# Moving the second half of a depthwise convolution from its own stage into the scan of the first half of the images

## The chip, the cores and the metric

The kernel runs on one core of a Trainium2 chip. The metric is device time in microseconds (us) for one execution: the median of three runs is 3259.85 us (3253.21 to 3263.72). TensorE (PE in the profile, with PEld for its weight loads) does the matrix products into PSUM, ScalarE (ACT) and VectorE (DVE) read PSUM and SBUF, GpSimd (POOL) works in SBUF, and SyncE (SP) issues most of the DMAs. "PEclk" is the TensorE clock that the throttle granted, as a share of full speed.

## The reference, cut to what matters

The input is 32 images of 96 channels, 56 by 56, in float32. Two layers follow each other.

```
# layer 0
h = depthwise_conv7x7(x) + conv_b
h = layernorm over channels (g, b)
x = x + layer_scale * (gelu(h @ w1 + b1) @ w2 + b2)
# layer 1
x  = silu(depthwise_conv5x5(x) + conv_b)              # "the second convolution"
d, B, C = split(x_proj_w @ x)                         # 6 + 4 + 4 rows
delta   = softplus(dt_w @ d + dt_b)
log_dA  = max(delta * A, log(1e-9))                   # 4 states per channel
P  = exp(cumsum(log_dA along the 3136 positions))
hs = P * cumsum(delta * B * x / max(P, 1e-9))
y  = sum over states of hs * C + x * Ds
```

The two layers meet only through the image: the scan of an image needs the second convolution of that image and of no other.

## The kernel before

The 32 images are two groups of 16 (g = 0 and 1). A convolution block (`conv`) is 4 channels of the 16 images of one group, so 24 blocks make one convolution of one group, and the blocks are numbered n = 0 to 95: 0 to 47 for the 7x7 convolution of both groups, 48 to 71 for the 5x5 convolution of group 0, 72 to 95 for that of group 1. A depthwise convolution is done on TensorE as products with banded matrices: the image rows lie on 32-partition quarters, and for each of the k + 1 column shifts `convolve` (L341) issues 8 products of 32 rows by 64 columns over up to 448 positions, on 4 row groups times 2 column groups of the array, so that a 5x5 block has 48 products (96 instructions in the profile, since each float32 product is two) into one PSUM slot of 4 banks. `bands` (L366) writes the banded matrices of a block on ACT from a table that is built once. `conv_load` (L400 for the 5x5) brings the block in with 8 DMAs on the SP queue; `conv` evicts on ACT, and `put2` (L439) writes the result to DRAM (`conv2_d`) with 4 DMAs on the POOL queue.

The stages follow each other on TensorE. First comes the 7x7 convolution of group 0. Then 56 units (u) of the channel MLP, two per 8 rows of images: `expand` (L569), GELU, `second` (L588) and `residual`, which writes its rows of `block_d`. The units of group 0 also carry the 7x7 convolution of group 1, one block per unit, and the units u = 30 to 49 of group 1 carry one 5x5 block of group 0 each (n = 48 to 67, "mixed" units); TAIL = 4 holds the last four back. After the last unit comes a stage of 28 blocks, n = 68 to 95, that holds nothing else ("the tail"). Then the scan runs, over 32 images with 6 units each (3 channel thirds g times 2 halves h of the columns), 192 units in all.

Each iteration i of the scan loop issues in program order, which every engine keeps:

```
load(p, s)      # SP: 12 DMAs; in two of 12 iterations (a pair of images)
prepare(b, s)   # i mod 6 = 5: project (24 products, px L831, xd); 0: delta (pz L848, softplus);
                # 1, 2: delta_x (POOL product L863, 4 DMAs on SP)
fetch(i+4)      # SP: u <- dx_d, 784 KB
spread(.., 0)   # i mod 6 = 3, 4: pk L879, bc L883 on ACT
decay(i+2)      # PE pd L901, ACT relu L906 twice, ACT exp L910 -> da
drive(i+2)      # POOL u <- u, bc (L915)
spread(.., 1)   # i mod 6 = 5, 0
scan(i)         # DVE L920, L924, L928
weigh(i-1)      # POOL da <- u, bc (L935)
gather(i-2)     # PE py L942, L947; ACT copy y L953; every third: 4 DMAs on SP
```

All products of the scan but none of its state go through one PSUM pool (`banks`) of 2 slots of 2 banks each; the other 4 banks hold the running product `run_t`. So TensorE can be at most two slots ahead of ACT, which empties every slot. The tiles `bc` have 3 buffers for each of the two kinds, `dx` two, `u` six, `da` five.

## Time and profile before

| | before |
|---|---|
| median of 3 runs | 3259.85 us |
| the profiled execution's own time | 3265.01 us |
| its span, first to last instruction | 3263.2 us |
| busy, share of the span: PE, DVE, ACT, POOL | 88%, 66%, 62%, 54% |
| last MLP product ends / tail runs on TensorE | 1296.2 us / 1296.2 to 1476.8 us |
| first scan instruction on DVE | 1511.3 us |
| scan unit 81 starts on DVE / last one starts | 2240.0 us / 3243.4 us |

The shares are means over stages of different kinds. Up to 1296 us TensorE is busy nearly all the time and VectorE is not; from 1511 us on VectorE is busy nearly all the time. The slices of the page show the two, and the windows and timelines of the trace show what happens inside a unit.

### The profile page before, as it was taken

Reading aid. Unit: us, or ns where it says so; the run is one execution under the profiler, and the core shown is the slowest. Engines: PE = TensorE matmul, PEld = TensorE weight load, DVE = VectorE, ACT = ScalarE, POOL = GpSimd, SP = SyncE. Lnnn points to the kernel's source line nnn. Section 1 sums busy time; section 2 is a strip of 40 time slices with the busy share of each in tenths; the row PEclk is TensorE's granted clock in tenths of the full one; section 3 lists DMA queues with packets and bytes.
Section 4 is the critical chain, followed back from the end, with each engine's and each line's share of the span. In section 5 each row is a group of like instructions: output and inputs, shape, how many; then the busy total and the mean of one; then the engine's idle time right before and its main releaser. Section 6 shows DMA issues by size and latency. Waiting matters only on the chain.

```text
span 3263.2 us, 65714 instructions
## 1 busy us (share of the span) xinstructions
PE 2855.5 (88%) x28044; PEld 1058.7 (32%) x28044; DVE 2138.3 (66%) x1226; ACT 2011.3 (62%) x1952; POOL 1760.3 (54%) x901
## 2 busy tenths in 40 slices
PE   8999999999999999887888887888787878887885
PEld 7654444444444444442222222222222222222221
DVE  6654333343121112004999999999999999999998
ACT  7765554444666665445766666666666666666673
POOL 2310111100111111335988898899888988898896
PEclk9999999999999999997788777877887878778786
DMA  8988666544777773997365546554655565556542
GB/s 193 254 244 222 186 183 185 166 129 126 202 206 203 202 200 98 279 275 199 119 179 147 148 149 178 148 151 146 178 149 142 155 175 142 143 163 159 157 156 72
DMA packets 363795, 563.63 MB, mean 173 GB/s; under 512 B 221904, under 2 KB 292576, under 8 KB 363504
## 3 DMA queue, kind: packets, MB, share of 16 engines
q1 hardware_dynamic: 336452, 432.37, 49.1%
q0 software_dynamic: 25424, 127.03, 13.1%
q8 instruction: 221, 3.62, 0.5%
q14 instruction: 70, 0.57, 0.1%
q10 hardware_dynamic: 1628, 0.04, 0.0%
HBM read 355.58 MB, written 203.69 MB: 171 GB/s over the span
## 4 chain that ended last, share of the span: by engine, by line
PE 51%; DVE 16%; ACT 9%; POOL 7%; DMA 7%; SPq 5%; issue 4%; POOLq 0%; DVEq 0%; ACTq 0%
PE pc L341 12%; PE ph L569 12%; PE po L588 12%; DVE u L928 6%; DVE run_t L920 6%; DVE run_t L924 3%; POOL da L935 3%; PE px L831 3%; PE py L947 3%; PE pz L848 3%; ACT da L906 3%; POOL u L915 3%; PE py L942 2%; ACT da L910 2%; PE pd L901 2%
## 5 line engine op out<-in xcount | busy, mean ns | idle before, releaser
L915 POOL TENSOR_TENSOR u<-u,bc 128x1568 f32<-128x1568 f32 x192 | 674.4, 3513 | 209.3 <-DMA u<-dx_d 209.3
L920 DVE TENSOR_TENSOR_SCAN run_t<-da,run_t 128x1568 f32<-128x1568 f32 x192 | 664.5, 3461 | 72.6 <-ACT da L910 54.0
L935 POOL TENSOR_TENSOR da<-u,bc 128x1568 f32<-128x1568 f32 x192 | 674.3, 3512 | 23.1 <-DVE u L928 21.0
L906 ACT ACTIVATE da<-pd,lift_t,a_t 128x784 f32<-128x784 f32 x384 | 378.4, 1003 | 73.1 <-PE pd L901 63.9
L901 PE MATMUL pd<-dl,rep_t 32*128 32x392 f32 x1536 | 388.6, 640 | 33.9 <-ACT bc L883 14.1
L569 PE MATMUL ph<-h,w1c_t 32*128 32x448 f32 x4032 | 398.0, 543 | 7.3 <-DVE o L600 3.8
L588 PE MATMUL po<-g,w_t 128*32 128x448 f32 x4032 | 390.4, 540 | 0.0
L942 PE MATMUL py<-xs,dsm_t 32*32 32x392 f32 x1536 | 250.2, 731 | 147.0 <-ACT bc L883 113.2
L341 PE MATMUL pc<-xc,we 32*64 32x432 f32 (+2 forms) x6912 | 359.3, 554 | 6.7 <-ACT we L366 4.3
L924 DVE SCALAR_TENSOR_TENSOR run_t<-run_t,u 128x1568 f32<-128x1568 f32 x192 | 345.6, 1800 | 21.8 <-POOL u L915 1.5
L575 ACT ACTIVATE g<-ph,b1p_t 128x1792 f32<-128x1792 f32 x168 | 294.5, 1754 | 98.8 <-PE ph L569 95.9
L879 PE MATMUL pk<-xd,pick_t 32*128 32x392 f32 x1024 | 266.0, 632 | 101.4 <-ACT y L953 85.6
L928 DVE TENSOR_TENSOR_SCAN u<-da,u,run_t 128x1568 f32<-128x1568 f32 x96 | 334.1, 3480 | 3.4
L555 DVE TENSOR_TENSOR h<-h,po 128x448 f32<-128x448 f32 x123 | 69.1, 617 | 405.6 <-PE po L588 308.0
L928 DVE TENSOR_TENSOR_SCAN u<-da,run_t 128x1568 f32<-128x1568 f32 x96 | 328.3, 3420 | 3.3
L439 POOL DMA_DIRECT2D conv_d<-ht x192 | 101.3, 535 | 408.6 <-ACT ht L446 268.2
L910 ACT ACTIVATE da<-da,lift_t 128x1568 f32<-128x1568 f32 x192 | 307.9, 1604 | 5.6
L947 PE MATMUL py<-da,sel_t 128*32 128x392 f32 x1536 | 246.7, 728 | 53.5 <-POOL da L935 53.4
L608 POOL DMA_DIRECT2D block_d<-o x112 | 60.2, 562 | 416.5 <-DVE o L600 395.4
L422 POOL DMA_DIRECT2D conv_d<-ht x96 | 57.1, 600 | 406.0 <-ACT ht L420 399.5
L953 ACT COPY y<-py 128x392 f32<-128x392 f32 x192 | 92.1, 480 | 296.3 <-PE py L947 227.0
L569 PEld LDWEIGHTS ph<-h,w1c_t 32*128 32x128 f32 x4032 | 198.8, 185 | 206.5 <-issue 167.3
(123 smaller groups left out, 3092.3 us busy)
## 6 DMA issues: line engine op xcount, KB each, us to landing
u<-dx_d SPq DMA_DIRECT2D x192, 784.0 KB, 5.2
conv_d<-ht POOLq DMA_DIRECT2D x96, 448.0 KB, 6.1
conv_d<-ht POOLq DMA_DIRECT2D x192, 224.0 KB, 5.7
h<-conv_d SPq DMA_DIRECT2D x336, 112.0 KB, 3.0
x<-in_x_dram SPq DMA_DIRECT2D x112, 336.0 KB, 8.6
block_d<-o POOLq DMA_DIRECT2D x112, 336.0 KB, 6.3
xs<-conv_d SPq DMA_DIRECT2D x384, 98.0 KB, 4.1
dx_d<-dx SPq DMA_DIRECT2D x256, 147.0 KB, 3.3
```

The lines of the kernel that those rows point to most:

```text
L341: pin(nc.tensor.matmul(pv[:, :, lo:hi], lhsT=wt[rows, j, k - d], rhs=xv[rows, j, :, lo + e : hi + e, s], start=(t == 0), stop=(t == k), ti ...
L569: pin(nc.tensor.matmul(ph[:, q, :TOK], lhsT=w1c_t[quarter(q), e, f * 128 : (f + 1) * 128], rhs=ht[quarter(q), e, s], start=(e == 0), stop= ...
L588: pin(nc.tensor.matmul(po[quarter(q), e, :TOK], lhsT=w2_t[:, f, e * PR : (e + 1) * PR], rhs=gts[u, f][:, q], start=(f == 0), stop=(f == 2) ...
L901: pin(nc.tensor.matmul(ps[:, j, :BK], lhsT=rep_t[quad(q)].rearrange("p c n -> p (c n)"), rhs=dls[b, h][quad(q), g], start=True, stop=True, ...
L906: pin(nc.scalar.activation(pair(da, a), ps[:, :, :BK], AF.Relu, bias=lift_t[:, 0:1], scale=a_t[:, g : g + 1],))
L910: pin(nc.scalar.activation(da, da, AF.Exp, bias=lift_t[:, 1:2], scale=1.0))
L915: pin(nc.gpsimd.tensor_mul(us[i], us[i], bcs[b, h, 0]))
L920: pin(nc.vector.tensor_tensor_scan(run_t[:, 1 : T + 1], da, zero, run_t[:, T : T + 1] if h else 1.0 / EPS, ALU.mult, ALU.add,))
L924: pin(nc.vector.scalar_tensor_tensor(run_t[:, :T], in0=run_t[:, 1 : T + 1], scalar=1.0, in1=ut, op0=ALU.min, op1=ALU.mult,))
L928: pin(nc.vector.tensor_tensor_scan(ut, da, run_t[:, :T], last["h"] if h else 0.0, ALU.mult, ALU.add))
L935: pin(nc.gpsimd.tensor_mul(das[i], us.pop(i), bcs[b, h, 1]))
L947: pin(nc.tensor.matmul(py[quad(j)], lhsT=sel_t, rhs=hc[:, j * BK : (j + 1) * BK], start=False, stop=True, tile_position=(0, j * PR),))
```

## The change

The constant TAIL goes away, so the MLP units u = 30 to 53 carry all 24 blocks of group 0. The tail is removed. The 24 blocks of group 1 (n = 72 to 95) are issued inside the scan of group 0, as 48 half blocks of two row groups each, at the end of the iterations with i mod 6 in 1, 2, 4 and, for even images, also 3. The first half of a block is copied out of PSUM (ACT), the second is evicted with SiLU, and SiLU is then applied to the first (ACT). The half blocks take their PSUM slot from the scan's `banks`. Their matrices are written to DRAM on the POOL queue when those of group 0 are made (the two groups have the same matrices), and each block's 393 KB come back by one SP DMA into a single buffer; the block's 8 loads and the 4 DMAs of its result are on the SP queue too. In the scan's loop the second `spread` comes one iteration later, `bc` has 2 buffers instead of 3 and `dx` one instead of two. Constants that only the first stages need move to a pool that is given back.

```diff
-XB, HB, TAIL = 4, 2, 4
+XB, HB = 4, 2
...
+    bands_d = [dram.tile([128, 2 * (K2 + 1) * 2 * PR], F32, name=f"bands_d{k}") for k in range(KB)]
...
-    def convolve(ps, xt, wt, k):
+    def convolve(ps, xt, wt, k, lanes=range(Q)):
...
-            for i in range(Q):
+            for i in lanes:
...
-                    pv = ps[j * 64 : (j + 1) * 64, i, :TOK].rearrange("p (b g) -> p b g", b=BI)
+                    pv = ps[j * 64 : (j + 1) * 64, i - lanes[0], :TOK].rearrange("p (b g) -> p b g", b=BI)
...
         wes[n] = t
+        if n >= half_n:
+            pin(nc.gpsimd.dma_start(bands_d[kb], t.rearrange("p j d m -> p (j d m)")))
...
-        mixed = 0 < u < half_u and n1 < half_n or u >= half_u + 2 and n2 < half_n + KB - TAIL
+        mixed = 0 < u < half_u and n1 < half_n or u >= half_u + 2 and n2 < half_n + KB
...
-    late = convs.enter_context(tc.tile_pool(name="late", bufs=1))
-    more += [late.tile([128, 2, COLS], F32, name=f"xd_{i}") for i in range(4)]
-    for t in more:
-        nc.vector.memset(t, 1.0)
-    last = half_n + KB
-    for n in range(n2, 2 * half_n):
-        ahead(n, last if n < last - XB else 2 * half_n)
-        conv(n)
...
-            dx = apool.tile([128, NG, BK], F32, name=f"dx_{k}", tag="dx")
+            dx = apool.tile([128, NG, BK], F32, name=f"dx_{k}", tag="dx", bufs=1)
...
-            t = pool.tile([128, T], F32, name=f"bc{i}_{b}_{h}", tag=f"bc{i}", bufs=3)
+            t = pool.tile([128, T], F32, name=f"bc{i}_{b}_{h}", tag=f"bc{i}")
...
+        xqs = [late.tile([128, 2, COLS], F32, name=f"xq_{i}") for i in range(2)]
+        blocks = range(half_n + KB, 2 * half_n)
+        halves = [(n, c) for n in blocks for c in range(2)]
...
+        def bring(n):
+            if n in blocks:
+                conv_load(n, xqs[n % 2])
+
+        def bring_bands(n):
+            if n in blocks:
+                t = late.tile([128, 2, K2 + 1, 2 * PR], F32, name=f"wq_{n}", tag="bands", bufs=1)
+                pin(nc.sync.dma_start(t.rearrange("p j d m -> p (j d m)"), bands_d[n % KB]))
+                wes[n] = t
+
+        def half_block(n, c):
+            ps = banks(f"pc_{n}_{c}")
+            convolve(ps, xqs[n % 2], wes[n], K2, range(2 * c, 2 * c + 2))
+            if c == 0:
+                hqs[n] = late.tile([128, Q, TOK], F32, name=f"hq_{n}", tag="ht", bufs=1)
+                pin(nc.scalar.copy(hqs[n][:, :2], ps[:, :, :TOK]))
+            else:
+                ht = hqs.pop(n)
+                pin(nc.scalar.activation(ht[:, 2:], ps[:, :, :TOK], AF.Silu))
+                pin(nc.scalar.activation(ht[:, :2], ht[:, :2], AF.Silu))
+                wes.pop(n)
+                coming.append((n + 2, n + 1))
+                leaving.append((n, ht))
...
+        bring_bands(blocks[0])
+        bring(blocks[0])
+        bring(blocks[1])
         for i in range(units + 3):
...
             if 0 <= i + 4 < units:
                 fetch(i + 4)
+            out_now, leaving[:] = leaving[:], []
+            if coming:
+                bring_bands(coming[0][1])
+                bring(coming.pop(0)[0])
...
-            b, s = divmod(i + 1, PER)
-            if i and b < B and s < 2:
+            b, s = divmod(i, PER)
+            if b < B and s < 2:
                 spread(b, s, 1)
-            if i == 0:
-                spread(0, 0, 1)
-                spread(0, 1, 1)
...
             if 0 <= i - 2 < units:
                 gather(i - 2)
+            for n, ht in out_now:
+                put2(n, ht, nc.sync)
+            b, s = divmod(i, PER)
+            if halves and (s in (1, 2, 4) or s == 3 and b % 2 == 0):
+                half_block(*halves.pop(0))
```

## The prediction

> **What bounds the kernel now.** I read the page's busy shares and slices first.
>
> ```profile
> PE 2855.5 (88%) x28044; PEld 1058.7 (32%) x28044; DVE 2138.3 (66%) x1226; ACT 2011.3 (62%) x1952; POOL 1760.3 (54%) x901
> PE   8999999999999999887888887888787878887885
> DVE  6654333343121112004999999999999999999998
> PEclk9999999999999999997788777877887878778786
> ```
>
> There are two regimes. Up to slice 19 TensorE is full at full clock; from 1511 us VectorE is full, and the clock falls. The windows of the scan's units 0 to 80 and 81 to 191 put numbers to it (columns: busy us of PE, PEld, DVE, ACT, POOL, each with its count; clock; DMA share; GB/s):
>
> ```profile
> 1511.00:2240.00 729.00, 600.75 (x3670) 162.65 (x3670) 705.55 (x244) 493.44 (x557) 637.22 (x189) 0.79 0.58 158
> 2240.00:3252.00 1012.00, 806.01 (x4900) 215.46 (x4900) 966.64 (x333) 657.95 (x740) 871.69 (x257) 0.79 0.53 150
> ```
>
> VectorE is busy 97% and 96% of the time, so a unit costs 9.0 to 9.1 us and an image (6 units) 54.4. But nothing else is loose: PE 82%, POOL 87%, ACT 68%. The waits show how near the others are.
>
> ```profile
> ACT y L953 <- PE py L947: 227.0, 117, 8.6
> POOL u L915 <- DMA u<-dx_d: 209.3, 31, 9.6
> PE py L942 <- ACT bc L883: 113.2, 62, 2.7
> PE pk L879 <- ACT y L953: 85.6, 45, 6.5
> DVE run_t L920 <- ACT da L910: 54.0, 24, 32.6
> PE py L947 <- POOL da L935: 53.4, 18, 6.1
> ```
>
> PE waits for ACT to empty a PSUM slot, and ACT for PE to fill one: a chain that goes to and fro over two slots. It waits for its pace-setter (POOL's da, which follows the scan) only 53 us in all on PE. How fast the chain goes when nothing holds it can be read from ACT's timeline, from the start of one exp (L910) to the next. For the six units of an image the distances that recur are 4.0, 5.9, 5.9, 9.7 (a px in between), 14.3 (a pz and both table loads) and 8.3 us: 48.1 us. So the chain has about 6 us of slack per image, and that is all the room the change has. A plain unit is ACT back to back:
>
> ```profile
> 2017.68 1.90 ACT L906 ACTIVATE da<-pd,lift_t,a_t 128x784 f32<-128x784 f32 x2 [0.51 <-PE pd L901]
> 2019.62 1.61 ACT L910 ACTIVATE da<-da,lift_t 128x1568 f32<-128x1568 f32 x1
> 2021.13 0.46 ACT L953 COPY y<-py 128x392 f32<-128x392 f32 x1
> ```
>
> **Part 1, the tail goes.** It runs from 1296.2 us (end of the last MLP product) to 1476.8, and the first scan instruction comes at 1511.3: 215.1 us from the MLP's end to the scan. Four of its 28 blocks become mixed units. PE's timeline of the MLP's last mixed unit and of the plain one after it:
>
> ```profile
> 1190.34 4.99 PE L341 MATMUL pc<-xc,we 32*64 32x448 f32 x96
> 1195.25 7.05 PE L569 MATMUL ph<-h,w1c_t 32*128 32x448 f32 x72
> 1202.13 0.91 PE L546 MATMUL po<-rstd_t,pickr_t 32*128 32x448 f32 x2
> 1202.97 6.97 PE L588 MATMUL po<-g,w_t 128*32 128x448 f32 x72
> 1209.87 7.05 PE L569 MATMUL ph<-h,w1c_t 32*128 32x448 f32 x72
> ```
>
> A block is 4.91 us there (1190.34 to 1195.25) in a full PE: 4 x 4.91 = 19.6 us. What remains between the MLP's end and the first scan is the loading of xs, project, delta, spread and decay. Before, it took 41.7 us from the first xs issue (1469.6) to 1511.3. The loads may have to wait until the last unit's o is written out, 12 us after the MLP (1308.2). I take 45 us, between 38 and 54. The scan then starts at 1296.2 + 19.6 + 45 = 1361, **150 us sooner** (141 to 157). The 24 matrix stores add 24 POOL issues of about 0.56 us in a stage where POOL is 15% busy: nothing; uncovered it would be 13 us.
>
> **Part 2, the half blocks.** A tile of the array takes its products one after another. ph has 72 instructions on four tiles, 18 in a row on each, in 6.88 us: 0.38 us per step. The whole pc block has 96 on eight tiles, 12 in a row, in 4.91: 0.41. A half block keeps two row groups, so 48 instructions on four tiles: still 12 in a row. It takes 4.6 to 4.9 us, as long as a whole block; I take 4.7 at full clock, and 4.7 / 0.79 = 5.9 at the scan's. That is 48 x 4.7 = 226 us of PE work in units 1 to 80, in place of 24 x 4.9 = 118.
>
> ACT adds per block one half copy and two half SiLUs (whole tiles took 1.65 and 1.68, so 0.84 each) and two table loads (1.28 each): 5.1 us, 2.5 per half block.
>
> The SP queue gets 13 issues per block (8 loads, one for the matrices, four of put2, which leave POOL): 312 at 0.43 to 0.53 us, some 150 us in about 930, with the 68 per pair of images that it has. By itself that fits, as do 2.2 MB per block, 57 GB/s on top of 158; what counts is the order, below. The two memsets of the new input tiles (1.55 us each on VectorE) lie in the 45 us of Part 1.
>
> Where does it lie? In a plain unit pc gets its slot when the second relu is gone and py is issued, some 4 us into the unit. The unit's exp and y pass under pc, so those 4.7 us come on top of the 4.0. The eviction after it finds the next unit's pd in the other slot waiting for the same ACT: a copy delays it by about 0.3, two SiLUs by about 1 more, and the exp's table load, where no pc covers it, by 1.28. Averaged: 0.8. The matrices have one buffer and can only be fetched when the second half's last product is done; they land about 5.2 us after issue (the median of the 784 KB u), and the next pc in a plain unit is ready after some 4. The result tile has one buffer too: 8 load issues (0.43 each) and put2's four lie before its landing (5.7), about 12 us after the SiLU's half block ended, while the next copy is ready after 9 to 11. In four images 4 of 7 blocks follow directly, and one of them finds the 12 xs loads (6.3 to 9.2 us) ahead on the SP queue. I put this at 7 us per four images, 0.5 per half block.
>
> So 6.0 us per half block, between 4.7 (all but the product hidden) and 9.5 (clock stays at 0.79: 5.9, ACT 1.6, DMA waits 2.0). With 3.5 per image the chain becomes 48.1 + 21.0 = **69.1 us per image** (64.6 to 81.4), well above VectorE's 53.8: VectorE waits. A busier PE may be granted more clock: px and pz (5.9 and 4.9 us for 48 instructions) would shrink to 4.2 each, and the lower end becomes 62. Units 0 to 80 are 13.5 images: 13.5 x 69.1 = 933 us against 729: **204 us lost** (108 to 370).
>
> **Part 3, the rest of the scan.** The later second spread takes about 2.5 us out of the longest stretch (px to pz) and puts it in a short one. With two bc buffers the first spread's eviction waits for the last drive on the buffer (POOL, issued one iteration before), and the relus queued behind it wait too; the weigh that gather waits for anyway follows on POOL 3.5 us later, so at worst 3 us per image. With one dx buffer POOL waits for the first dx's DMAs (3.3 us to landing, plus queueing behind xs loads) before the second, and behind it wait drive and weigh, but POOL already stands 209 us for u. I take +10 us for the 18.5 images after unit 81, between -15 and +40.
>
> **Sum.** Against the profiled execution (3265.0 us with 1.8 outside its span, 5.2 above the median): -150 + 204 + 10 = +64, so 3329. Against the median: 3260 + 64 = 3324 us.
>
> Break-even is at (729 + 150 - 10) / 13.5 = 64.4 us per image, or 4.7 us per half block: precisely the product alone. All else would have to be hidden.
>
> **Two rules of the Trainium skill.** Row: from 2030 to 2044 us the clock was 0.52 with PE busy 11.0 of 14 us and no gap over 2.7 us. "TensorE: Matmul & The Clock Gate" (HAM oscillation) asks only that PE not idle for more than about 3.4 us; the row disagrees. By the rule the new chain would run at full clock: 45.5 + 21 = 66.5 us per image, and 3289 us. Row: pc to ph (32x64 to 32x128 tiles) passes at 1195.25 without a gap. "TensorEngine Tiling (Array Packing)" (Key Properties) says that a change of tiling mode drains the array, which speaks against putting pc between py and pd; at an estimated 0.16 us (a product's 0.54 less its step of 0.38), two per half block, it would add 15 us.
>
> **Rivals.**
> *Faster:* PE at full clock (px and pz at 4.2: chain 45.5) with ACT and DMA hidden: 45.5 + 3.5 x 4.9 = 62.6 per image, 845 us for units 0 to 80: 3260 - 150 + 116 + 5 = 3231, with a quiet second half. For it: the tail ran at 0.86 to 0.97 in its windows of 50 us, and pc fills the very gaps that dropped the clock. Against it: 227 us of ACT waiting for PE and 199 of PE waiting for ACT (113.2 + 85.6) already show a chain that does not overlap. It decides below 64.4 us per image.
> *Much slower:* the single buffers and the SP queue. Each block pays its matrix fetch and put2 in full, and the clock stays at 0.79: 8 us per half block, 76.1 per image: +298 - 150 + 20 gives 3428. For it: SP already waits 481 us for y and 552 for da and u. Against: fetches are issued four units ahead.
> *Hidden:* the half blocks fit under VectorE and the whole 150 stays: 3120. Against it stands the 6 us of slack.
>
> **How the numbers follow.** Forecast (3275 to 3390) 0.56, much slower 0.13, faster 0.24, hidden 0.03, nothing 0.04. Measurement of this kernel tells about 0.3% from no change. Faster 0.27, same 0.04, slower 0.69. The range leaves out the hidden case and the ends of the two outer ones: 3205 to 3440; the forecast's own is 3275 to 3390.
>
> **What would show it.** Right: the scan starts near 1361; pc of 48 takes 4.7 to 6 us; DVE is below 85% busy up to unit 80 at some 11.5 us per unit and back at 9.1 after, with the wait for the exp (L910) grown from 54 to some 200 us; ACT's silus find their table loaded under pc. Wrong: DVE stays above 93% in units 1 to 80; or POOL or SP, not the PE and ACT chain, ends DVE's waits; or the second part of the scan changes by over 40 us.

## The result, and the profile after

The changed kernel takes 3547.5 us (median of four runs, 3542.64 to 3562.04) against 3261.78 us for the kernel before beside it: a ratio of 1.0887, with a 95% interval of 1.0845 to 1.0928. It is slower by 286 us where 64 were forecast. The profiled execution spans 3541.7 us, 278.5 more than before.

The page of the changed kernel, busy shares and three rows of the slices:

```profile
PE 3141.2 (89%) x28044; PEld 1126.1 (32%) x28044; DVE 2134.9 (60%) x1224; ACT 2064.1 (58%) x2015; POOL 1728.0 (49%) x829
PE   8999999999999988988998899899887878877885
DVE  6654333431111114555666656565799999999998
PEclk9999999999999996666676857566677777777786
```

TensorE runs the same 28044 products, but is busy 286 us longer (2855.5 before). The stretch in which VectorE is half idle, slices 15 to 27, is the stretch in which the granted clock shows 5 to 8, mostly 6. The windows of units 0 to 80 and 81 to 191 (span, then busy us of PE, PEld, DVE, ACT, POOL, clock, DMA share, GB/s):

```profile
1364.00:2501.00 1137.00, 1006.35 (x5856) 302.53 (x5856) 705.08 (x243) 610.66 (x668) 640.39 (x188) 0.66 0.56 147
2501.00:3541.00 1040.00, 824.01 (x5024) 228.94 (x5024) 967.01 (x334) 661.06 (x749) 875.46 (x258) 0.75 0.54 148
```

The scan starts at 1363.5 us, 148 sooner than before (1511.3). Units 0 to 80 take 1137.6 us in place of 728.7: 409 lost. The rest takes 1040.6 in place of 1023.2: 17 lost. -148 + 409 + 17 = 278, the difference of the spans. So all of the question lies in the first window, and there the row can be read as a sum. Of TensorE's 1006.35 us the half blocks have this (the same window, instructions that write pc only: PE, PEld, ACT):

```profile
1364.00:2501.00 1137.00, 361.16 (x2208) 123.41 (x2208) 41.93 (x46) 0.66 0.56 147
```

That is 46 half blocks at 7.85 us. The scan's own products took 1006.35 - 361.16 = 645.2 us, where they took 600.75 before, and TensorE was idle for 130.7 us, where it was idle for 128.3. So the lost 409 us are 361 of half blocks, 44 of scan products that became slower, and 2 of idle time: the half blocks filled none of TensorE's gaps, on balance, and all of it is TensorE's busy time.

The waits (us in total, times, longest) that answer to those shown of before:

```profile
DVE run_t L911 <- ACT da L901: 487.7, 76, 40.6
POOL dx L854 <- DMA dx_d<-dx: 244.5, 31, 13.9
ACT y L944 <- PE py L938: 203.2, 107, 8.5
ACT hq L983 <- PE pc L343: 202.5, 23, 18.0
PE py L933 <- ACT bc L874: 109.1, 62, 2.7
PE pc L343 <- DMA wq<-bands_d: 27.3, 3, 10.1
```

VectorE's wait for the exp grew from 54.0 to 487.7 us. ACT waits 202.5 us for first halves alone: it isn't late, it stands behind TensorE. Only 27 us of TensorE's idle time are put down to the matrices' DMA.

Why a half block takes 7.85 us is seen in TensorE's timeline around 2070 us, and in the window of the same stretch:

```profile
2072.91 2.77 PE L892 MATMUL pd<-dl,rep_t 32*128 32x392 f32 x8
2075.69 1.53 PE L933 MATMUL py<-xs,dsm_t 32*32 32x392 f32 x8
2077.15 1.53 PE L938 MATMUL py<-da,sel_t 128*32 128x392 f32 x8
2078.61 9.02 PE L343 MATMUL pc<-xq,wq 32*64 32x448 f32 x48
2087.57 2.78 PE L870 MATMUL pk<-xd,pick_t 32*128 32x392 f32 x8
```
```profile
2051.00:2125.00 74.00, 71.68 (x348) 20.82 (x352) 43.49 (x15) 32.13 (x35) 41.20 (x12) 0.50 0.63 156
```

TensorE is busy 71.68 of 74 us, and yet it has half the clock all through. A half block takes 9.02 us there, and 4.96 at full clock (2025.08 us). The records of the granted clock know only these two levels, and between the first and the last record each lasts a whole number of steps of 3.41 us. In units 0 to 80 of before, half clock adds up to 311 us, and its longest stretch is 13.7 us; in the changed kernel it is 768 us, with twelve stretches over 25 us, the longest 85.3.

ACT's timeline in the same place, to be held against the plain unit shown before:

```profile
2076.77 1.60 ACT L901 ACTIVATE da<-da,lift_t 128x1568 f32<-128x1568 f32 x1
2078.75 0.49 ACT L944 COPY y<-py 128x392 f32<-128x392 f32 x1 [0.38 <-DMA xs<-conv_d]
2079.26 1.28 ACT L986 ACT_TABLE_LOAD   x1
2087.71 0.92 ACT L986 ACTIVATE hq<-pc 128x896 f32<-128x896 f32 x1 [7.17 <-PE pc L343]
2088.52 0.94 ACT L987 ACTIVATE hq<-hq 128x896 f32<-128x896 f32 x1
...
2094.01 1.28 ACT L901 ACT_TABLE_LOAD   x1
```

SiLU's table is loaded while pc runs, as the forecast had it, and ACT then waits 7.17 us more for pc. The exp's table load at 2094.01 is not covered.

### The profile page after: what moved, and what is told of

Same layout as the page of the kernel before. It is cut to its first block, busy times and chain, and to the rows that moved or that the text cites. A ratio compares the mean times of both kernels' runs of the same rounds, so it can differ in the third digit from the quotient of the medians.

```text
span 3541.7 us, 65641 instructions
## 1 busy us (share of the span) xinstructions
PE 3141.2 (89%) x28044; PEld 1126.1 (32%) x28044; DVE 2134.9 (60%) x1224; ACT 2064.1 (58%) x2015; POOL 1728.0 (49%) x829
## 4 chain that ended last, share of the span: by engine, by line
PE 65%; ACT 15%; DVE 5%; SPq 5%; issue 4%; DMA 4%; POOL 2%; POOLq 0%; ACTq 0%; DVEq 0%
PE pc L343 20%; PE po L585 11%; PE ph L566 11%; ACT da L897 5%; PE pd L892 5%; PE px L822 4%; PE py L933 4%; PE py L938 4%; ACT da L901 3%; PE pk L870 3%; SPq L803 2%; ACT dl L846 2%; DVE u L919 2%; ACT bc L874 2%; DVE run_t L911 2%
## 5 line engine op out<-in xcount | busy, mean ns | idle before, releaser
L911 DVE TENSOR_TENSOR_SCAN run_t<-da,run_t 128x1568 f32<-128x1568 f32 x192 | 664.5, 3461 | 500.5 <-ACT da L901 487.7
L892 PE MATMUL pd<-dl,rep_t 32*128 32x392 f32 x1536 | 405.4, 719 | 75.3 <-ACT bc L874 61.1
L343 PE MATMUL pc<-xq,wq 32*64 32x432 f32 (+1 forms) x2304 | 379.2, 825 | 37.3 <-DMA wq<-bands_d 27.3
L854 POOL TENSOR_TENSOR dx<-dl,xs 128x1176 f32<-128x1176 f32 x64 | 189.5, 2960 | 416.0 <-DMA dx_d<-dx 244.5
L933 PE MATMUL py<-xs,dsm_t 32*32 32x392 f32 x1536 | 262.6, 766 | 138.4 <-ACT bc L874 109.1
L919 DVE TENSOR_TENSOR_SCAN u<-da,u,run_t 128x1568 f32<-128x1568 f32 x96 | 334.1, 3480 | 3.4
L919 DVE TENSOR_TENSOR_SCAN u<-da,run_t 128x1568 f32<-128x1568 f32 x96 | 328.4, 3420 | 3.3
L870 PE MATMUL pk<-xd,pick_t 32*128 32x392 f32 x1024 | 276.5, 700 | 29.5 <-ACT da L897 25.2
L938 PE MATMUL py<-da,sel_t 128*32 128x392 f32 x1536 | 254.2, 749 | 25.5 <-POOL da L926 25.5
L892 PEld LDWEIGHTS pd<-dl,rep_t 32*128 32x128 f32 x1536 | 153.3, 244 | 340.8 <-ACT bc L874 141.8
L422 POOL DMA_DIRECT2D conv_d<-ht x96 | 57.3, 602 | 405.8 <-ACT ht L420 395.5
```

The costliest lines, as they stand in the source:

```text
L343: pin(nc.tensor.matmul(pv[:, :, lo:hi], lhsT=wt[rows, j, k - d], rhs=xv[rows, j, :, lo + e : hi + e, s], start=(t == 0), stop=(t == k), ti ...
L892: pin(nc.tensor.matmul(ps[:, j, :BK], lhsT=rep_t[quad(q)].rearrange("p c n -> p (c n)"), rhs=dls[b, h][quad(q), g], start=True, stop=True, ...
L911: pin(nc.vector.tensor_tensor_scan(run_t[:, 1 : T + 1], da, zero, run_t[:, T : T + 1] if h else 1.0 / EPS, ALU.mult, ALU.add,))
L919: pin(nc.vector.tensor_tensor_scan(ut, da, run_t[:, :T], last["h"] if h else 0.0, ALU.mult, ALU.add))
L933: pin(nc.tensor.matmul(py[quad(j)], lhsT=dsm_t[quad(j), g], rhs=tokens(b, h, quad(j), g), start=True, stop=False, tile_position=(j * PR, j ...
L938: pin(nc.tensor.matmul(py[quad(j)], lhsT=sel_t, rhs=hc[:, j * BK : (j + 1) * BK], start=False, stop=True, tile_position=(0, j * PR),))
```

## Experiments

The theory was that the products of the half blocks, which keep two of TensorE's four row groups, are what holds the clock down; the rivals were the loads (SP queue, single buffers), the table loads and evictions on ACT, and the changed order of the rest of the scan. A single run is good to some 10 us (the four runs of the changed kernel lie within 20).

**What of the inserted work costs.** Whole blocks in place of half blocks: 24 blocks, eight tiles on four row groups each, into both slots, SiLU straight out of PSUM, at i mod 6 = 2 and 4 of images 0 to 11.

```diff
-            if halves and (s in (1, 2, 4) or s == 3 and b % 2 == 0):
-                half_block(*halves.pop(0))
+            if waiting and s in (2, 4):
+                whole_block(waiting.pop(0))
```

> The 24 blocks of the second half are issued whole, two per image (i mod 6 = 2 and 4, images 0 to 11), on all eight 32x64 tiles of the array at once, each taking both PSUM slots of the scan; their loads, the fetch of their matrices, the single buffers and the SP queue stay as in the changed kernel, and only one pass of SiLU per half is left. Theory A (a half block fills only half of the array; work of that kind does not get the full clock granted, so pc takes about 8 us instead of 4.7 and the scan's own products slow down with it): pc takes 5 to 6 us per whole block, the granted clock in the scan of the first half is above 0.72 instead of 0.65, a block adds 8 to 10 us to the chain, and the time is 3230 to 3340 us. Theory B (the SP queue and the single buffers): the order of the DMAs is the same, so the time stays above 3450 us. Theory C (SiLU and table loads on ScalarE): the table loads stay, the copies go, so 3480 us or more.

Measured: 3289.16 us (3285.08 to 3296.62), ratio 1.0085 (1.0059 to 1.0112). The window of units 0 to 80 of this run, first all instructions, then pc alone:

```profile
1364.00:2270.00 906.00, 744.27 (x5952) 245.28 (x5952) 704.49 (x243) 590.02 (x648) 640.55 (x188) 0.81 0.71 185
1364.00:2270.00 906.00, 141.94 (x2304) 80.16 (x2304) 41.41 (x48) 0.81 0.71 185
```

The clock is 0.81 in place of 0.66, a whole block takes 5.9 us where two halves took 15.7, and the scan's own products are back at 602.3 us. Of the 286 us, 258 are gone with the same loads, the same table loads and the same buffers. But the run changes the number of products per us, the number of evictions and the rows at once, so it says what is to be looked for, not which of these it is.

Then the rivals by themselves. Without the loads: only the first two blocks are loaded and one set of matrices fetched; the other blocks are computed from these.

```diff
-            if n in blocks:
+            if n in blocks[:2]:
                 conv_load(n, xqs[n % 2])
...
-            if n in blocks:
+            if n in blocks[1:]:
+                wes[n] = wes["kept"]
+            elif n in blocks:
```

> The changed kernel, but only the first two blocks of the second half are loaded and only the first one's matrices are fetched; all blocks reuse them (this leaves out the data of the other 22 blocks). The results are still written out. Theory A (half array, low clock): only the waits of pc for matrices and loads go (37 us of PE idle time ahead of pc in the profile), so 3490 to 3540 us. Theory B (SP queue and single buffers): most of the loss of units 0 to 80 beyond the prediction goes, so below 3400 us.

Measured: 3502.97 us, 44 less than the changed kernel; the clock in units 0 to 80 is 0.68.

Without SiLU: copies in its place, so its table loads and those that bring the exp's table back after it are left out.

```diff
-                pin(nc.scalar.activation(ht[:, 2:], ps[:, :, :TOK], AF.Silu))
-                pin(nc.scalar.activation(ht[:, :2], ht[:, :2], AF.Silu))
+                pin(nc.scalar.copy(ht[:, 2:], ps[:, :, :TOK]))
+                pin(nc.scalar.copy(ht[:, :2], ht[:, :2]))
```

> The changed kernel, but the half blocks of the second half are copied instead of put through SiLU (this leaves out SiLU for half of the images), so the two table loads per block go and the ACT work itself stays. Theory A: the table loads lie mostly under pc, at most 24 x 2.57 = 62 us are saved, so 3480 to 3545 us. Theory C (ScalarE's tables set the pace): below 3420 us.

Measured: 3468.68 us, 79 less; the clock is 0.75. That is more than the 62 us that the table loads themselves could give by the first of the two forecasts, and well short of the second. Both edits together:

> The changed kernel with copies in place of SiLU and with only the first two blocks' loads and one matrix fetch (outputs of the other blocks are left out). Alone, copies gave 79 us and no loads gave 44. Theory (what is left is the product on a clock that is not won back): 3425 to 3455, pc 6.2 to 6.8 us per half block, clock 0.72 to 0.77, still 165 us or more above the kernel before. Rival (tables and DMA waits make the gaps in which the clock is lost): without them the clock holds, pc is 5 to 5.5 us per half block, 3300 to 3380.

Measured: 3434.02 us. The window of units 0 to 80 of this run, all instructions, then pc alone:

```profile
1364.00:2401.00 1037.00, 921.27 (x5856) 270.62 (x5856) 705.13 (x243) 550.22 (x622) 641.08 (x188) 0.73 0.50 133
1364.00:2401.00 1037.00, 301.87 (x2208) 98.16 (x2208) 41.69 (x46) 0.73 0.50 133
```

Loads and tables together account for 113 us. With neither of them 175 us of the loss are still there, and a half block still takes 6.6 us, so the larger part has another cause. The table below sets the runs side by side: the window of units 0 to 80, TensorE's busy time in it, split in pc and the rest, and its idle time.

| kernel | window us | PE busy | pc | scan's own | PE idle | clock |
|---|---|---|---|---|---|---|
| before | 729 | 600.75 | 0 | 600.75 | 128 | 0.79 |
| changed | 1137 | 1006.35 | 361.16 | 645.2 | 131 | 0.66 |
| no loads | 1101 | 990.72 | 349.40 | 641.3 | 110 | 0.68 |
| no SiLU | 1065 | 910.16 | 296.21 | 614.0 | 155 | 0.75 |
| neither | 1037 | 921.27 | 301.87 | 619.4 | 116 | 0.73 |
| whole blocks | 906 | 744.27 | 141.94 | 602.3 | 162 | 0.81 |

The loads are worth 20 us of idle time and 16 of TensorE's busy time. The table loads are worth nothing in idle time; what goes with them is 96 us of TensorE's busy time (65 in pc, 31 in the scan's own), that is, clock. That the holes which the table loads make are where the clock is lost is a reading of this row; no run isolates it.

**Where the clock comes from.** The tail of the kernel before is the cleanest place for this, because TensorE does nothing else there. First its blocks issued as two halves of two row groups, one after the other:

```diff
-        convolve(ps, source(n), wes.pop(n), k)
+        wt = wes.pop(n)
+        if n >= half_n + KB - TAIL:
+            for c in range(2):
+                convolve(ps, source(n), wt, k, range(2 * c, 2 * c + 2))
...
```

> The kernel before, with its tail of 28 blocks in place, but each of these blocks issues its products as two halves of two row groups one after the other (same products, same slot, same evictions). Nothing else is disturbed, so this measures the half width by itself. Theory A: the clock of the tail falls from 0.86 to 0.97 to 0.5 to 0.7 and a block takes 14 to 18 us, the tail 400 to 500 us, and the time is 3480 to 3590 us. Theory A' (half width only halves the number of tiles at work; TensorE is busy without gaps, so the clock stays full): a block takes 9.4 to 9.8 us, the tail about 275 us, and the time is about 3355 us.

Then both halves on the same two row groups, so that they cannot overlap (the second half reads the first's rows, so its output is not the convolution's):

```diff
-                rows = slice(i * PR, (i + 1) * PR)
+                q = i if len(lanes) == Q else i % 2
+                rows = slice(q * PR, (q + 1) * PR)
...
-                        tile_position=(i * PR, j * 64),
+                        tile_position=(q * PR, j * 64),
```

> The kernel before with its tail of 28 blocks, each issued as two halves, and both halves on the same two row groups of the array (the second half computes the first half's rows again, so this leaves out half of the rows of the second half of the images). So only four tiles, 64 of the 128 rows of the array, are ever at work in the tail, with as many products as before. Theory A, sharpened by the run with halves on different rows (whose halves overlapped, PE 100% busy at a clock of 1.00): products on half of the rows do not win the full clock back once it has been lost. The waits for the first blocks of the second half drop the clock, as in the kernel before, and then a block takes about 18 us instead of 9.4: the tail is 400 to 490 us, its clock 0.5 to 0.65, the time 3480 to 3570 us. Theory A' (a TensorE without gaps gets the full clock whatever its tiles): 28 x 9.4 = 263 us, clock above 0.9, the time about 3345 us.

Measured: 3262.68 us, no change, and 3338.05 us. For the first run neither forecast came true, since both took it that the halves would not overlap; in the second the rival's did (about 3345), the theory's (3480 to 3570) did not. The windows of the tail, of the first run and of the second:

```profile
1298.00:1470.00 172.00, 172.00 (x2517) 78.20 (x2513) 8.08 (x7) 85.46 (x80) 54.85 (x104) 1.00 0.87 262
```
```profile
1296.00:1550.00 254.00, 254.00 (x2581) 100.35 (x2576) 8.09 (x7) 88.64 (x82) 56.98 (x108) 1.00 0.76 194
```

In the first the halves overlap across the row groups (6.1 us per block). In the second they follow each other at 9.4 us per block, and the clock is 1.00 for 254 us. So four tiles on two row groups *hold* a full clock as long as TensorE has no gap: a theory by which they always run at half clock falls here. What is left is that they can't win back a clock that has been lost. The second run can't show this, because nothing in its tail makes TensorE wait. For this a gap is needed. 200 tiny operations on ACT ahead of one block's matrices make one, once with the blocks of before and once with those of the run just shown:

```diff
         ahead(n, last if n < last - XB else 2 * half_n)
+        if n == last + 4:
+            for _ in range(200):
+                table(AF.Silu)
         conv(n)
```

> The kernel before, with 200 tiny operations on ScalarE ahead of the matrices of one block in the middle of the tail, so that TensorE runs dry once for 20 us or more; all blocks keep their 8 tiles on all four row groups. Theory (a full clock, once lost, is not won back by products on half the rows, but is by products on all of them): the clock falls to about 0.5 in the gap and is back above 0.95 within about 15 us of products after it; blocks after it take 5 to 6 us each; time 3262 plus the gap, some 3280 to 3310. Rival (any TensorE without gaps wins the clock back): the same. Rival (the clock depends on what ScalarE or the power of the whole core does): no rule for the return.

> The same gap in the tail, where the blocks are issued as two halves one after another on the same two row groups (9.4 us per block at full clock, 3338 us without the gap). Theory: before the gap the clock is 1.00 and a block takes 9.4 us; after it the clock stays near 0.5 for tens of us although TensorE has no gaps, blocks take up to 18 us, and the time is 3420 to 3560. Rival (any TensorE without gaps wins the clock back within some 15 us): 9.4 us per block again after the gap, and 3355 to 3390.

Measured: 3284.75 us and 3519.59 us. TensorE idles 41.05 us at a stretch in the first and 33.57 in the second. The windows of the gap and after, with the eight-tile blocks:

```profile
1358.00:1400.00 42.00, 0.95 (x13) 0.14 (x3) 0.00 (x0) 36.70 (x172) 0.61 (x2) 0.55 0.40 65
1400.00:1410.00 10.00, 10.00 (x137) 8.27 (x145) 0.00 (x0) 5.14 (x5) 3.61 (x7) 0.67 0.71 197
1410.00:1420.00 10.00, 10.00 (x213) 9.19 (x204) 0.00 (x0) 7.03 (x8) 4.21 (x8) 1.00 0.97 253
```

and with the blocks on two row groups:

```profile
1386.00:1430.00 44.00, 10.65 (x109) 4.12 (x100) 0.00 (x0) 38.38 (x181) 0.30 (x1) 0.67 0.24 42
1430.00:1742.00 312.00, 311.78 (x1709) 157.97 (x1713) 0.00 (x0) 57.15 (x54) 39.77 (x76) 0.50 0.43 104
```

This is the cause in one line: 311.78 us busy out of 312, and the clock stays at 0.50 to the end of the tail, while eight tiles have it back within 10 us. In the same run the clock comes back at 1752.2 us, 4 us after the scan's first products, px, begin; they lie on all four row groups. TensorE's timeline and the windows there:

```profile
1748.08 6.64 PE L840 MATMUL px<-xs,bcw_t 32*32 32x392 f32 x48 [1.85 <-issue]
1748.00:1752.00 4.00, 3.92 (x25) 1.33 (x29) 0.06 (x1) 0.00 (x0) 2.11 (x4) 0.50 0.62 151
1752.00:1756.00 4.00, 2.85 (x32) 0.91 (x28) 0.00 (x0) 1.07 (x2) 0.00 (x0) 0.98 0.30 82
```

It could still be the number of tiles. So the same gap once more, with four tiles on all four row groups and one column half, two passes per block (the second pass takes the place of the other half's output, which is left out):

```diff
-                for j in range(2):
+                for j in range(2) if js is None else [js]:
+                    m = 0 if js is not None else j
...
-                        tile_position=(i * PR, j * 64),
+                        tile_position=(i * PR, m * 64),
```

> The kernel before with the gap in the tail, and blocks issued as two passes one after another on the same four tiles, as in the run with 4 tiles, but now the four tiles are on all four row groups and one column half (the other half's output is left out, and ScalarE evicts in two parts). Theory 'rows' (the clock comes back with the rows in use): 9.4 us per block, the clock is back at 1.00 within some 15 us after the gap, time 3365 to 3400. Theory 'tiles' (it takes eight busy tiles, or a certain number of products per us): the clock stays at 0.50 after the gap as with two row groups, about 18 us per block, time 3500 to 3540.

Measured: 3373.58 us. The windows:

```profile
1386.00:1430.00 44.00, 6.74 (x59) 3.56 (x55) 0.00 (x0) 38.94 (x165) 2.21 (x5) 0.60 0.21 42
1430.00:1440.00 10.00, 10.00 (x94) 8.71 (x90) 0.00 (x0) 3.29 (x4) 2.03 (x4) 0.87 0.37 98
1440.00:1450.00 10.00, 10.00 (x107) 8.81 (x103) 0.00 (x0) 5.53 (x5) 2.12 (x4) 1.00 0.86 190
1450.00:1590.00 140.00, 140.00 (x1430) 123.63 (x1426) 0.00 (x0) 73.76 (x60) 31.74 (x60) 1.00 0.80 199
```

The same number of tiles, and at full clock the same 10.2 products per us as in the run without the gap (1430 in 140 us here, 2581 in 254 us there), and the clock is back. It is the row groups in use, not the number of tiles. Nor is it the share of the array or the PSUM banks: the px products above have four tiles of 32 by 32, a quarter of the array where the two row groups fill half, and they write one PSUM bank at a time where a half block on two row groups writes two.

**Does that hold inside the scan?** Two runs. In the first 12 products of 128 rows by 128 columns over 64 positions go ahead of each half block; they are added work.

```diff
             ps = banks(f"pc_{n}_{c}")
+            for r in range(12):
+                pin(nc.tensor.matmul(
+                    ps[:, r % 2, TOK : TOK + 64], lhsT=xqs[n % 2][:, 0, :128], rhs=xqs[n % 2][:, 1, :64],
+                    start=True, stop=True,
+                ))
```

> The changed kernel with 12 extra products of 128 rows by 128 columns over 64 positions ahead of each half block, into columns of its PSUM slot that nobody reads; nothing else changes. They add 2 to 4 us of TensorE work to each of 48 half blocks, 100 to 190 us in all. Theory A: products on all rows win the full clock back, so the half block behind them takes about 5 us instead of 7.9, the clock of units 1 to 80 rises from 0.66 to above 0.8, and the time stays near that of the changed kernel or falls: 3420 to 3580 us. Theories B and C, or any in which only the amount of work on the chain counts: 3640 to 3740 us, with pc as long as before.

Measured: 3638.89 us, 91 more than the changed kernel. A half block came down to 305.59 / 46 = 6.6 us and the clock rose to 0.73, but the added products took 184.6 us themselves. Neither forecast fits: the theory's 3420 to 3580 us was too low, and the rival's had pc as long as before. Nor do the added products bring the clock back themselves: of the 28 steps of 3.41 us at half clock in which they take over half of TensorE's time, none was the last of its stretch. They use all rows, but with only 64 positions for each weight load; loading weights is busy for 171.67 of their 178.79 us in the window 1364 to 2600 us. So all rows alone are not enough, and why the half blocks became shorter this run does not show.

The second run has the blocks halved the other way at the same 48 places: four tiles on all four row groups and one column half, into both slots.

```diff
-            ps = banks(f"pc_{n}_{c}")
-            convolve(ps, xqs[n % 2], wes[n], K2, range(2 * c, 2 * c + 2))
+            ps = [banks(f"pc_{n}_{c}_{a}") for a in range(2)]
+            rows = slice(c * 64, (c + 1) * 64)
+            convolve(ps, xqs[n % 2], wes[n], K2, js=[c])
```

> The changed kernel with its blocks halved the other way: each half block is 48 products on four tiles as before, but on all four row groups and one column half, into both PSUM slots, at the same 48 places. Theory (the rows in use decide whether a lost clock comes back): the clock from 1364 us to unit 81 rises from 0.66 to 0.76 to 0.85, and a half block takes 5.2 to 6.3 us in place of 7.85, some 100 us in all; the scan's own products are up to 44 us shorter; ScalarE has five half-width evictions of a block in place of three, about 62 us more: 3430 to 3490. Rival (the clock is lost for another reason, and the tail's finding does not carry over): the clock stays at 0.64 to 0.69, the evictions come on top, 3585 to 3620.

Measured: 3479.29 us. Units 0 to 80, all instructions, then pc alone:

```profile
1364.00:2438.00 1074.00, 879.61 (x5856) 288.77 (x5848) 704.33 (x243) 664.72 (x714) 640.91 (x188) 0.81 0.60 156
1364.00:2438.00 1074.00, 283.49 (x2208) 133.34 (x2208) 78.59 (x92) 0.81 0.60 156
```

The clock is 0.81 in place of 0.66, a half block 6.16 us in place of 7.85, and the scan's own products take 596.1 us in place of 645.2; no stretch at half clock is longer than 17.1 us. That is 78 + 49 = 127 us of TensorE time, with the same number of products, table loads and DMAs. 64 us come back as idle time, so that 68 are gained in all; with it go five evictions per block (117.6 us on ACT in place of 63.6) and both slots taken, which no run separates. So the way the block was halved costs the changed kernel about 127 us of TensorE's time. What remains is the work itself, put in a place where nothing hides it, in halves that each take as long as a whole block (46 halves 283.49 us, 24 whole blocks 141.94).

The records show the same thing in the changed kernel itself. The half clock of the row at 2051 to 2125 us ends at 2125.07, 2.9 us after a px has taken over from pc (TensorE's timeline and the window after):

```profile
2117.71 4.54 PE L343 MATMUL pc<-xq,wq 32*64 32x432 f32 x24
2122.18 6.19 PE L822 MATMUL px<-xs,bcw_t 32*32 32x392 f32 x48
2125.00:2135.00 10.00, 8.71 (x79) 2.16 (x72) 0.68 (x1) 6.40 (x7) 0.00 (x0) 1.00 1.00 243
```

And it is not pc alone. The scan's own pd and pk also put their products on two row groups per slot (L892 and L870); py, px and pz use all four. In units 0 to 80 of the changed kernel, 171 steps of 3.41 us at half clock have TensorE busy for at least 95%. In the 21 after which the clock was back, pc, pd and pk took at most 35% of TensorE's time; in the 150 after which it stayed down, at least 31%, and 84% on average. In the kernel before, 33 such steps have at most 31% of pd and pk, and 5 have at least 39%. Busy time counts as well: of the 53 steps in which TensorE was busy for less than 95%, one was the last of its stretch.

Whole blocks whose halves are issued one after the other ask whether the order of issue matters:

```diff
-            convolve(ps, xqs[n % 2], wes.pop(n), K2)
+            wt = wes.pop(n)
+            for c in range(2):
+                convolve(ps[c], xqs[n % 2], wt, K2, range(2 * c, 2 * c + 2))
```

> 24 whole blocks at the places of the run with whole blocks (3289 us), but each as two half blocks one after another on different row groups, into the two slots. If the halves overlap on the array as they do in the tail, a block takes 6 to 7 us and the time is 3285 to 3330: then what counts is that all four row groups have work in one stretch, not the order of issue. If TensorE takes them one after another, or the clock falls as in the changed kernel, a block takes 9.4 to 16 us and the time is 3370 to 3530.

Measured: 3356.43 us, between the two forecasts. A block takes 236.06 / 24 = 9.8 us (8.31 at 1838.64 us): the halves do not overlap as they did in the tail. But the clock is 0.79 and the scan's own products take 600.6 us, so halves that use all four row groups one right after the other do not pull the clock down.

**The rest of the scan.** The kernel before with two bc buffers, one dx buffer and the later second spread, and nothing else:

```diff
-            dx = apool.tile([128, NG, BK], F32, name=f"dx_{k}", tag="dx")
+            dx = apool.tile([128, NG, BK], F32, name=f"dx_{k}", tag="dx", bufs=1)
...
-            t = pool.tile([128, T], F32, name=f"bc{i}_{b}_{h}", tag=f"bc{i}", bufs=3)
+            t = pool.tile([128, T], F32, name=f"bc{i}_{b}_{h}", tag=f"bc{i}")
...
-            b, s = divmod(i + 1, PER)
-            if i and b < B and s < 2:
+            b, s = divmod(i, PER)
+            if b < B and s < 2:
                 spread(b, s, 1)
```

> The kernel before with only the smaller buffers and the moved spread of the change: two bc buffers of each kind, one dx buffer, the second spread one iteration later; the tail and all else as before. This is Part 3 of the prediction by itself: for all 32 images instead of the 18.5 after unit 81, so +17 us by the prediction's central value (10 x 32 / 18.5), between -26 and +69; from the two profiles (units 81 to 191 took 17 us longer in the changed kernel) about +30 us.

Measured: 3268.28 us, ratio 1.0025 (1.0013 to 1.0038), 8 us. Its waits show the trade that the forecast named:

```profile
POOL dx L863 <- DMA dx_d<-dx: 207.4, 31, 10.1
ACT bc L883 <- POOL u L915: 89.4, 14, 7.4
```

POOL now stands 207.4 us for the dx DMAs where it stood 209.3 for u. In its profile the scan starts 10 us later (1521.0 us; POOL waits 4.9 us for the DMAs of the first dx before it can make the second), units 0 to 80 take 729 us as before, and the rest is 8 us shorter: by this profile the price lies ahead of the scan and not in it. The same buffer beside whole blocks, where the SP queue is fuller: whole blocks with two dx buffers.

> The version with whole blocks, with two dx buffers again as in the kernel before (bc stays at two). If POOL's wait for the one dx buffer (240 us of idle time in the profile of the whole blocks) matters where ScalarE and TensorE do not set the pace, that is after the last block, this takes 5 to 25 us off 3289 us: 3264 to 3284 us. If that wait only takes the place of POOL's wait for u, as the prediction had it, 3284 to 3292 us.

Measured: 3271.34 us, ratio 1.0037 (1.002 to 1.0055), 18 us less than with one; so there the one buffer does not only take the place of another wait.

**A version that gains.** Whole blocks with two dx buffers, three bc buffers of the first kind, and the 24 blocks spread over 14 images:

```diff
-            if waiting and s in (2, 4):
+            if waiting and (s == 4 or s == 2 and (b % 2 or b < 6)):
```

> Whole blocks as in the run with two dx buffers (3271 us), spread over 14 images in place of 12, one or two per image so that none falls where the xs loads of a pair are issued, and the first kind of bc with 3 buffers. Theory (what is left is the product, 5 to 6 us per block, plus two SiLUs and a table load): 24 blocks at about 9 us less the slack of 14 images at 6 us makes 130 us in place of the 150 that the tail cost: 3235 to 3265, at or just below the kernel before. Rival (a whole block also blocks both slots, and every stall of the chain counts): 3270 to 3290, no better than before.

Measured: 3256.28 us, ratio 0.9994 (0.9979 to 1.0009): not to be told from the kernel before. Last, only one whole block per image (i mod 6 = 4, 14 blocks), and the other ten left in a tail of 14 blocks:

```diff
+    for n in range(n2, half_n + KB + 10):
+        ahead(n, half_n + KB if n < half_n + KB - XB else half_n + KB + 10)
+        conv(n)
...
-        blocks = range(half_n + KB, 2 * half_n)
+        blocks = range(half_n + KB + 10, 2 * half_n)
...
-            if waiting and (s == 4 or s == 2 and (b % 2 or b < 6)):
+            if waiting and s == 4:
```

> Ten of the second half's 24 blocks stay in a tail of 14 blocks, and 14 run as whole blocks inside the scan, one per image (i mod 6 = 4), with two dx buffers and three bc buffers of the first kind. Theory (an image has 6 us of slack, and a whole block costs about 9): the tail is some 88 us shorter, 14 blocks cost 3 us each beyond the slack, 42 us, and the fewer bc buffers some 5: 3205 to 3230, ratio 0.983 to 0.991. Rival (every inserted block is paid in full, no slack): 14 blocks at 9 us take 126 us, 3290 to 3310.

Measured: 3227.78 us (3220.0 to 3231.64), ratio 0.9907 (0.989 to 0.9923), about 30 us faster than the kernel before. Its windows of units 0 to 80 and after:

```profile
1431.00:2208.00 777.00, 650.26 (x4896) 193.22 (x4896) 705.19 (x243) 543.81 (x606) 642.35 (x190) 0.84 0.70 186
2208.00:3218.00 1010.00, 810.04 (x5024) 222.65 (x5024) 967.33 (x334) 661.67 (x748) 873.43 (x257) 0.77 0.54 152
```

The scan starts at 1431.4, 80 us sooner, and units 0 to 80 take 48 us more than before, with 78.5 us of pc in them: 13 blocks at 6.0 us, which cost 3.7 us apiece. That is less than their product, but not because they fill gaps: TensorE is idle for 127 us, as before (128). The scan's own products take 571.8 us in place of 600.75, at a clock of 0.84 in place of 0.79; 13 of these 29 us also appear in the run with the smaller buffers alone (587.5), where the clock is 0.77, and what makes up the others was not separated. The second window is 13 us shorter than before's in this profile; what shortens it no run shows.

## Why the prediction was wrong

**Part 1 was right.** The scan starts at 1363.5, forecast 1361 (150 sooner, measured 148). A block in a mixed unit takes what the forecast took, in TensorE's timeline of the changed kernel:

```profile
1209.80 4.99 PE L343 MATMUL pc<-xc,we 32*64 32x448 f32 x96
1214.72 7.05 PE L566 MATMUL ph<-h,w1c_t 32*128 32x448 f32 x72
```

4.92 us from the one to the other. From the MLP's end (1315.7) to the scan 47.8 us passed, forecast 45.

**Part 3 was right in size, its reason not shown.** +10 forecast for the rest, +17 measured. The run of this part alone is 8 us slower in all, but by its profile the rest of the scan is not longer there, so the smaller buffers by themselves do not explain the 17.

**Part 2 is the step that failed, and in it the term of the product.** Its loss of 204 us was made of 47 half blocks (13.5 images of 3.5) at 4.7 us, 222, of ACT and DMA at 1.3 each, 61, and of 80 us of slack to be used up. Measured until unit 81: 361 us of product, 139 more than forecast; 44 us by which the scan's own products grew, of which the sum had nothing; and 2 us of idle time, where 61 - 80 = -19 was forecast, 21 more. 139 + 44 + 21 = 204, and 204 + 204 is the 409 within a us. Of the smaller terms the DMA waits were of the right size: by the run without loads they are 20 us of idle time, forecast 0.5 x 47 = 24. ACT's term and the slack were not measured one by one; together the three were to shorten TensorE's idle time by 19 us and left it as it was.

The wrong sentences are "I take 4.7 at full clock, and 4.7 / 0.79 = 5.9 at the scan's", with these as the two ends of the term, and "A busier PE may be granted more clock". TensorE did become busier (88% of the window in place of 82%), and the clock fell to 0.66. The end of the range should have been the half clock: 4.7 / 0.5 = 9.4, against 9.02 measured. A mean clock of 0.79 isn't a property of the stage; it is a mix of two levels, and the inserted products changed the mix. With 4.7 / 0.5 and the other terms in the middle the sum is 204 + 222 = 426 us, so the 409 would have been inside the range (in part by luck, because 9.4 throughout makes up for the 44 us that the sum lacked). By the middle of the two ends the forecast would have been some 110 us higher.

**The break-even was right as an idea, wrong as a hope.** 64.4 us per image were needed, 84.3 came out (1137.6 / 13.5). At 64.4 units 0 to 80 take 869 us. With 24 whole blocks they took 907, with 24 spread over 14 images 873 (and that kernel was not to be told from the one before), with 14 blocks 777.

**The rivals.** "Faster" lived on the sentence that pc fills the very gaps that dropped the clock. TensorE's idle time was 128 us before and 131 after. "Much slower" had the right size of the product (8 us per half block, 7.85 measured), but through single buffers, the SP queue and a clock of 0.79: without the loads 44 us go, so its cause is a small part of what happened, and its 3428 was still 120 too low.

**The two rules.** The clock rule gave 3289 and missed by 258 us; the row of 2030 to 2044 us had spoken against it, and it was the row that was right. The forecast then used the rule's direction all the same, a busier PE for a better clock. What the 312 us at 0.50 say of the rule stands in the last section. The drain at a change of tiles was not tested by itself.

**What was to show it.** Right: the start of the scan, VectorE below 85% (705 of 1137 us, 62%), SiLU's table loaded under pc, the second part within 40 us. Wrong: pc of 48 between 4.7 and 6 us (7.85), 11.5 us per unit (14.0), and the wait for the exp at 200 us (487.7).

## What to carry to other kernels

A product that is inserted into a stage has two prices, one at each level of the clock, and the range must reach to the one at half clock; then count which row groups it uses, because work that leaves half of TensorE's rows idle does not bring a lost clock back and makes its neighbours slower too. A block that had to be cut to fit a buffer was better cut by columns than by rows here, and better not cut at all. Work moved under another stage must cost less there than in its own stage: here one whole block per image did (48 us more in units 0 to 80, 80 us less ahead of the scan), and 24 blocks in 12 to 14 images did not. Whether the scan's own pd and pk would gain from all four row groups was not tried.

## What the runs showed of the hardware

The granted clock is not a matter of busy time alone. TensorE without a gap kept half clock for 312 us with products on two of four row groups, and kept full clock for 254 us with the same products when it had not been lost before. After gaps of 41 and 37 us, products on all four row groups had it back within 10 us, with eight tiles and with four. In units 0 to 80 of the changed kernel a step of 3.41 us with TensorE busy for 95% or more brought the clock back only where pc, pd and pk, the products on two row groups, took at most 35% of it. All rows are not enough by themselves: products of 128 rows over 64 positions, one weight load each, brought it back in none of 28 steps. So the same instruction takes 4.96 or 9.02 us by what ran before it.

"TensorE: Matmul & The Clock Gate" of the Trainium skill (Part 1, the HAM clock gate) says that some 3.4 us of sustained busy time are enough to reach the full clock. The runs with all row groups agree in kind: the eight-tile run was back at full clock some 7 us after its gap, the four-tile run some 5. The run with two row groups does not: 312 us of sustained busy time were not enough, and the measurement decides. What the gate counts was not seen, only that it tells these cases apart.
